# VectorE transposes head 6 as well in tiles 0 to 6, and layer 1's relu moves into the ring of block buffers

## The chip, the cores and the metric

The kernel runs on one core of one Trainium2 chip. The time is device microseconds (us) of one launch. A core has TensorE (PE: matmuls and transposes by matmul), VectorE (DVE), ScalarE (ACT), GpSimd (POOL) and SyncE (SP, which here only issues transfers), each with its own queue of instructions that it runs in order. They wait for one another through semaphores. On-chip memory is SBUF, and PSUM, where TensorE writes.

## The reference: two graph layers

There are 16 graphs of 1024 nodes with 256 features, and an integer matrix `adj` for each. Layer 0 is masked attention with 8 heads of 32 features, layer 1 is attention with a bilinear score and a leaky relu. Cut to what matters:

```
h = maximum(layernorm(x), 0)
Q, K, V = heads(h @ Wq.T + bq), heads(h @ Wk.T + bk), heads(h @ Wv.T + bv)
attn = softmax(where(adj == 0, -inf, Q @ K.T * SCALE))      # 8 heads, 1024 x 1024 each
x = x + (attn @ V) @ Wo.T + bo
h = maximum(layernorm(x), 0)
e = leaky_relu((h * a_0) @ h.T, 0.2)                         # a_1.. for adj == 2, 3, 4
x = x + softmax(where(adj == 1, e, -9e15)) @ h
```

## The kernel before

**Tiles and steps.** A graph is cut into 8 tiles of 128 rows (`t` = 0 to 7), so there are 128 tiles. The order of the work is written out by hand (lines 834 to 973). One step `s` of the loop works on three stages at once: `now`, layer 0 for tile `s`; `edge`, layer 1 for the tile 9 places back; `piece`, norm and projections for the tile 9 places ahead. A step has eight places, `h` = 0 to 7, and each engine's queue gets its instructions in the order of the calls.

**One head.** At place `h` the scores of head `h` are made by two matmuls of 128x512 (`scores`, L460) into one of two PSUM areas, `sides[0]` for heads 0, 1, 2, 3, 5 and 7 and `sides[1]` for 4 and 6. Layer 1's scores of the step also go to `sides[1]`. VectorE then masks the scores, finds the row's extreme and writes them to an SBUF buffer `p` (`softmax_max`, L472). At the next place ScalarE takes the exponential (`softmax_exp`, L489), at the place after that the 128x1024 tile is transposed into `pT`. Last, `combine(g)` (L525) multiplies the transposes of four heads with the values: group 0 at place 7 of the same step, group 1 (heads 4 to 7) at place 3 of the next step. Its 64 matmuls go round the four heads, so its third one already needs head 6.

**Two ways to transpose.** `turn` (L491) lets TensorE do it: eight 128x128 transposes (L589) into PSUM, and two copies out of it (L590), by ScalarE for heads 2, 3, 6, 7. `turn_blocks` (L497) lets VectorE transpose 32x32 blocks (L381) into a buffer `blocks`, and `place_blocks` (L386) issues four transfers of 128 KB on SP's queue, which put the blocks in their places in `pT`. The table `BY_BLOCKS` (L28) and `MIXED` (L27) say which heads of a tile go by blocks: heads 0, 1, 4, 5 in tiles 1 to 6, heads 4 and 5 in tile 0, heads 0 and 1 in tile 7. Layer 1's tile always goes by blocks (L686, L689).

**The order of the keys.** The block way wants a row's columns in another order inside a chunk of 128 than the other way. Keys and values of heads 0, 1, 4, 5 lie in that order already. Where a head's way differs from `MIXED`, `softmax_exp` (L481 to L488) takes a second buffer from the ring of `p` and the exponential reorders as it writes.

**Place 0 and place 1**, which the change touches: at place 0 of a step `turning` is the previous tile and `th` is 6. TensorE's order there is scores of head 0 (L460), the eight transposes of head 6 (L589), layer 1's first half (L625, L631); at place 1 scores of head 1, transposes of head 7, L564 and L267; then scores of head 2. VectorE's order is L472 of head 0, the block transposition of layer 1 (L381), L472 of head 1. SP's order is the transfers of head 4 and of head 5 (from places 6 and 7 of the step before), with L551 between them, then those of layer 1, then those of head 0.

**Rings.** A tag with `bufs=n` is a ring: a new tile takes a buffer over from an older one, and its first instruction waits until the older tile's last use is over. `p` has four, `blocks` three, `pT` seven, and `less` (L662, which holds layer 1's relu from L663 until GpSimd subtracts it in L674) one of its own.

Of the kernel before, what the change touches and what calls it, by code (L numbers as in the profile page):

```python
# [8 lines left out]
F32 = mybir.dt.float32  # L9
# [8 lines left out]
P = 128  # L18
HEADS = 8
HD = 32  # L20
# [4 lines left out]
NEG_INF = -9000000000000000.0  # L25
MASKED = -1e30
MIXED = (0, 1, 4, 5)  # L27
BY_BLOCKS = {7: (0, 1), 0: (4, 5)}  # L28


def by_blocks(t):
    return BY_BLOCKS.get(t, MIXED)

# [14 lines left out]
def gnn_kernel(  # L48
# [19 lines left out]
    B, N, D = x.shape  # L68
    NT = N // P
# [3 lines left out]
    NB = P // HD  # L73
# [10 lines left out]
    work = ctx.enter_context(tc.tile_pool(name="work", bufs=2))  # L84
# [103 lines left out]
    class Piece:  # L188
# [11 lines left out]
        def buffer(self, i, shape, dtype=F32):  # L200
            tag = self.tags[i]
            if tag == "pT":
                return ptp.tile(shape, dtype, tag=tag, name=tag)
            bufs = {"p": 4, "blocks": 3, "halves": 2 if self.n == 1 else 4, "qt": 2, "xin": 2}.get(tag, 1)
            return work.tile(shape, dtype, tag=tag, name=tag, bufs=bufs)

        def load(self, queue=nc.gpsimd):
# [169 lines left out]
        return rows.rearrange("(k b) n -> b k n", b=NB)  # L377

    def blocks_of(p):
        blocks = work.tile([P, NB, NT, HD], F32, tag="blocks", bufs=3)  # L380
        nc.vector.transpose(blocks.rearrange("p b j q -> p j b q"), p)  # L381
        return blocks.rearrange("p b j q -> p b (j q)")

# [31 lines left out]
    class Attend:  # L415
# [81 lines left out]
        def turn_blocks(self, h):  # L497
            self.blocks = blocks_of(self.probs[h][0])
# [94 lines left out]
    class Edges:  # L593
# [65 lines left out]
        def bend(self):  # L659

            if not self.last:
                self.less = work.tile([P, N], F32, tag="less", name="less", bufs=1)  # L662
                nc.scalar.activation(self.less, self.sel, AF.Relu, scale=1 - 1 / SLOPE)  # L663

        def leak(self):
# [20 lines left out]
        def turn_blocks(self):  # L686
            self.blocks = blocks_of(self.sel)
# [370 lines left out]
```

## Time and profile before

| what | us |
|---|---|
| median of 3 runs | 3093.83 (3088.1 to 3098.82) |
| the profiled execution's own time | 3096.04 |
| its span in the profile | 3093.7 |
| PE busy | 2966.1 (96%) |
| ACT busy | 2652.6 (86%) |
| DVE busy | 2517.3 (81%) |
| POOL busy | 2170.7 (70%) |

The profile records one execution. "Busy" is the time in which an engine had an instruction running; each row of a group of instructions gives the count, the busy time, the mean of one, and the idle time of the engine just before them with what ended it. The waits view adds up such idle time by who waited for whom. The timeline lists instructions in order of time with start and duration. Matmuls overlap each other, so their pace is read from start to start and not from the duration. SP's rows are the time it took to issue a transfer; when the data landed is recorded apart.

### The profile page before, as it was taken

To read this page: it belongs to the slowest core of one execution; us is meant where nothing else is said; L and a number is where in the kernel's file an instruction comes from. 1 tells how busy PE (TensorE), PEld (TensorE's weight loads), DVE (VectorE), ACT (ScalarE), POOL (GpSimd) and SP (SyncE) were. 2 spreads that over 40 slices of the span, in tenths; PEclk is the share of its full clock that TensorE was granted. 3 is DMA by queue.
4 is the path that set the end of the run, shared out by engine and by line. 5 is a ranking of instruction groups with operands and counts; after the bars stand their busy time and mean duration, and the time that the engine had idled before them with its cause. 6 is when DMAs were issued, how large, how long until landed. Compare 5 with 4: busy or idle time off the path is not lost. (4 is left out here: it accounts for less than half of the span.)

```text
span 3093.7 us, 96257 instructions
## 1 busy us (share of the span) xinstructions
PE 2966.1 (96%) x36722; PEld 2230.0 (72%) x36722; DVE 2517.3 (81%) x4455; ACT 2652.6 (86%) x5157; POOL 2170.7 (70%) x2995
## 2 busy tenths in 40 slices
PE   6889999999999999999999999999999999999997
PEld 3667777777777777777777777777777777777663
DVE  3777888888887888888888888888888888888884
ACT  3888988988998988988888898988888888898872
POOL 2666777777777777777777777777777777776542
PEclk8999999999999999999999999999999999999999
DMA  5676777777777777777867777777777867777653
GB/s 202 206 218 216 225 243 230 249 214 235 236 224 251 218 237 236 225 244 230 256 209 236 235 227 253 219 240 233 222 244 226 261 209 231 239 224 236 193 163 99
DMA packets 597828, 695.68 MB, mean 225 GB/s; under 512 B 63280, under 2 KB 528560, under 8 KB 597360
## 3 DMA queue, kind: packets, MB, share of 16 engines
q1 hardware_dynamic: 528288, 477.29, 51.6%
q0 software_dynamic: 66960, 210.04, 20.9%
q8 instruction: 295, 4.83, 0.7%
q10 hardware_dynamic: 2112, 2.10, 0.2%
q14 instruction: 173, 1.42, 0.1%
HBM read 252.98 MB, written 134.22 MB: 125 GB/s over the span
## 5 line engine op out<-in xcount | busy, mean ns | idle before, releaser
L472 DVE CUSTOM_DVE_ANT_0 p<-s,neg 128x1024 f32<-128x1024 f32 x1024 | 1236.2, 1208 | 238.1 <-PE s L460 191.8
L489 ACT ACTIVATE p<-p,nmx 128x1024 f32<-128x1024 f32 x1024 | 1249.4, 1223 | 146.2 <-DVE nmx L472 143.0
L460 PE MATMUL s<-k,qt 128*128 128x512 f32 x2048 | 760.5, 452 | 34.7 <-DMA qt<-qd 15.0
L590 ACT COPY pT<-trp 128x512 f32<-128x512 f32 x1024 | 548.8, 590 | 91.8 <-PE trp L589 91.6
L589 PE MATMUL trp<-ident,p 128*128 128x128 f32 x4608 | 604.4, 274 | 3.7 <-ACT pT L590 1.5
L589 PEld LDWEIGHTS trp<-ident,p 128*128 128x128 f32 x4608 | 531.7, 140 | 102.3 <-issue 10.9
L381 DVE STREAM_TRANSPOSE blocks<-p 128x1024 f32<-128x1024 f32 x456 | 564.5, 1238 | 13.5 <-ACT p L678 10.6
L525 PE MATMUL acc<-pT,v 128*32 128x128 f32 x16384 | 532.9, 275 | 37.5 <-ACT recT L519 25.8
L525 PEld LDWEIGHTS acc<-pT,v 128*32 128x32 f32 x16384 | 452.4, 110 | 148.3 <-ACT recT L519 80.8
L440 POOL TENSOR_SCALAR neg<-adj 128x1024 bf16<-128x1024 int32 x128 | 467.7, 3654 | 81.4 <-ACT neg L452 72.2
L696 PE MATMUL acc<-h,pT 128*32 128x256 f32 x8192 | 493.0, 382 | 7.9 <-DVE ot L705 7.8
L460 PEld LDWEIGHTS s<-k,qt 128*128 128x128 f32 x2048 | 322.6, 191 | 129.4 <-issue 44.3
L696 PEld LDWEIGHTS acc<-h,pT 128*32 128x32 f32 x8192 | 241.0, 109 | 210.2 <-issue 62.7
L674 POOL TENSOR_TENSOR sel<-sel,less 128x1024 f32<-128x1024 f32 x120 | 286.7, 2389 | 70.3 <-ACT less L663 49.2
L631 PE MATMUL s<-h1T,ha 128*128 128x512 f32 (+2 forms) x744 | 272.8, 490 | 2.6 <-ACT h1T L568 0.5
L672 POOL TENSOR_SCALAR less<-top 128x1 f32<-128x1 f32 x120 | 31.6, 264 | 275.4 <-DVE top L654 275.4
L324 POOL DMA_DIRECT2D qd<-halves x240 | 177.0, 777 | 58.7 <-POOL halves L314 31.7
L489 ACT ACTIVATION_READ_ACCUMULATOR p<-p,nmx 128x1 f32 x1024 | 206.2, 201 | 0.0
L509 POOL COPY wide<-rec 128x256 f32<-128x256 f32 x128 | 53.7, 419 | 210.5 <-DVE rec L507 210.5
L330 POOL DMA_DIRECT2D kd<-halves x240 | 171.7, 764 | 35.4 <-POOL halves L314 35.4
L314 POOL TENSOR_TENSOR halves<-full,halves 128x256 fp32r<-128x256 f32 x240 | 176.5, 736 | 20.6
L631 PEld LDWEIGHTS s<-h1T,ha 128*128 128x128 f32 x744 | 126.6, 190 | 70.6 <-issue 45.2
(121 smaller groups left out, 4322.6 us busy)
## 6 DMA issues: line engine op xcount, KB each, us to landing
pT<-blocks SPq DMA_DIRECT2D x2304, 128.0 KB, 3.5
k<-kd SPq DMA_DIRECT2D x128, 512.0 KB, 7.3
qt<-qd SPq DMA_DIRECT2D x128, 512.0 KB, 4.5
adj<-in_adj POOLq DMA_DIRECT2D x127, 512.0 KB, 4.9
qd<-halves POOLq DMA_DIRECT2D x240, 256.0 KB, 2.8
kd<-halves POOLq DMA_DIRECT2D x240, 128.0 KB, 4.0
xb<-in_x POOLq DMA_DIRECT2D x128, 128.0 KB, 4.2
x1d<-x SPq DMA_DIRECT2D x128, 128.0 KB, 3.9
```

Of the source, the lines that this page charges most:

```text
L324: nc.gpsimd.dma_start(out=qds[self.b][self.first, oc].rearrange("p u w n -> p u (w n)"), in_=halves.unsqueeze(1).to_broadcast([P, 2, 2 * P]),)
L381: nc.vector.transpose(blocks.rearrange("p b j q -> p j b q"), p)
L440: nc.gpsimd.tensor_scalar(self.neg, self.adj, 0.0, MASKED, ALU.is_equal, ALU.mult)
L460: nc.tensor.matmul(self.ps[:, cols], lhsT=self.qt[:, h, :], rhs=keysets[self.b][h][:, cols], start=True, stop=True,)
L472: nc.vector.tensor_tensor_reduce(out=p, in0=sides[h in (4, 6)], in1=self.neg, scale=-SCALE, scalar=FLOOR, op0=ALU.add, op1=ALU.min, accum_ ...
L489: nc.scalar.activation(to, of, AF.Exp, bias=nmx, scale=-1.0, accum_out=self.sums[:, h : h + 1])
L525: nc.tensor.matmul(sums_place[r * HD : (r + 1) * HD, g * P : (g + 1) * P], lhsT=vs[self.b][:, j, place_of(h) : place_of(h) + HD], rhs=self ...
L589: nc.tensor.transpose(tr[:, j, :], p[:, jj * P : (jj + 1) * P], ident)
L590: copy(pT[:, half * 4 : half * 4 + 4, :], tr)
L631: nc.tensor.matmul(self.side[:, cols], lhsT=self.ha[:, c, :], rhs=h1T[:, c, cols], start=(c == 0), stop=(c == NC - 1),)
L674: nc.gpsimd.tensor_tensor(self.sel, self.sel, self.less, ALU.subtract)
L696: nc.tensor.matmul(sums_place[a * HD : (a + 1) * HD, :], lhsT=self.pT[:, j, a], rhs=h1s[self.b][:, j, :], start=(j == 0), stop=(j == NT - 1),)
```

## The change

Head 6 of tiles 0 to 6 of each graph is transposed by VectorE in blocks. Head 6 is not in `MIXED`, so its exponential now writes to a second `p` buffer in the other order. The relu of layer 1 loses its own buffer and takes its place in the ring `blocks`, which has four buffers in place of three, so the memory used is the same.

```diff
-BY_BLOCKS = {7: (0, 1), 0: (4, 5)}
+BY_BLOCKS = {7: (0, 1), 0: (4, 5, 6), 1: (0, 1, 4, 5, 6), 2: (0, 1, 4, 5, 6), 3: (0, 1, 4, 5, 6), 4: (0, 1, 4, 5, 6), 5: (0, 1, 4, 5, 6), 6: (0, 1, 4, 5, 6)}
...
-            bufs = {"p": 4, "blocks": 3, "halves": 2 if self.n == 1 else 4, "qt": 2, "xin": 2}.get(tag, 1)
+            bufs = {"p": 4, "blocks": 4, "halves": 2 if self.n == 1 else 4, "qt": 2, "xin": 2}.get(tag, 1)
...
-        blocks = work.tile([P, NB, NT, HD], F32, tag="blocks", bufs=3)
+        blocks = work.tile([P, NB, NT, HD], F32, tag="blocks", bufs=4)
...
-                self.less = work.tile([P, N], F32, tag="less", name="less", bufs=1)
+                self.less = work.tile([P, N], F32, tag="blocks", name="less", bufs=4)
```

In the built queues, 112 groups of eight transposes and their 224 copies on ScalarE are gone (7 tiles of 16 graphs), and VectorE has 112 more block transpositions and SP 448 more transfers. At place 0 the new transposition stands on VectorE between L472 of head 0 and layer 1's block transposition, and on SP the new transfers stand between those of head 5 and those of layer 1.

## The prediction

> **What bounds the kernel now.** I read the page's busy times and groups, then the waits, then the timeline of one step, engine by engine. The groups that the change moves, on the page (count, busy us, mean ns, idle before them and what ended it):
>
> ```profile
> PE 2966.1 (96%) x36722; PEld 2230.0 (72%) x36722; DVE 2517.3 (81%) x4455; ACT 2652.6 (86%) x5157; POOL 2170.7 (70%) x2995
> ...
> L489 ACT ACTIVATE p<-p,nmx 128x1024 f32<-128x1024 f32 x1024 | 1249.4, 1223 | 146.2 <-DVE nmx L472 143.0
> ...
> L590 ACT COPY pT<-trp 128x512 f32<-128x512 f32 x1024 | 548.8, 590 | 91.8 <-PE trp L589 91.6
> L589 PE MATMUL trp<-ident,p 128*128 128x128 f32 x4608 | 604.4, 274 | 3.7 <-ACT pT L590 1.5
> ...
> L381 DVE STREAM_TRANSPOSE blocks<-p 128x1024 f32<-128x1024 f32 x456 | 564.5, 1238 | 13.5 <-ACT p L678 10.6
> ```
>
> PE is busy 96% and hardly waits: it sets the pace, and the change takes work from it. What that is worth depends on the place the work is taken from, so I look at the start of one step of tile t = 5, first on PE (start, duration):
>
> ```profile
> 1461.62 0.73 PE L460 MATMUL s<-k,qt 128*128 128x512 f32 x2
> 1462.19 1.04 PE L589 MATMUL trp<-ident,p 128*128 128x128 f32 x8
> 1463.06 0.60 PE L625 MATMUL s<-ident,mirror 128*128 128x128 f32 x4
> 1463.77 0.73 PE L460 MATMUL s<-k,qt 128*128 128x512 f32 x2
> ...
> 1466.24 0.71 PE L460 MATMUL s<-k,qt 128*128 128x512 f32 x2
> ...
> 1470.24 2.33 PE L525 MATMUL acc<-pT,v 128*32 128x128 f32 x64
> ```
>
> The row L589 at 1462.19 goes; it holds PE for 0.87 us, start to start. The three L460 are the scores of heads 0, 1 and 2, all into the same PSUM area. VectorE over the same time:
>
> ```profile
> 1461.05 1.24 DVE L381 STREAM_TRANSPOSE blocks<-p 128x1024 f32<-128x1024 f32 x1
> 1462.48 1.23 DVE L472 CUSTOM_DVE_ANT_0 p<-s,neg 128x1024 f32<-128x1024 f32 x1 [0.19 <-issue]
> ...
> 1463.63 1.24 DVE L381 STREAM_TRANSPOSE blocks<-sel 128x1024 f32<-128x1024 f32 x1
> 1464.80 1.19 DVE L472 CUSTOM_DVE_ANT_0 p<-s,neg 128x1024 f32<-128x1024 f32 x1
> ```
>
> L472 of head 0 ends at 1463.71, and the scores of head 1 start at 1463.77: they must not overwrite what VectorE still reads. PE's weight load shows that this is a wait already:
>
> ```profile
> 1463.77 0.30 PEld L460 LDWEIGHTS s<-k,qt 128*128 128x128 f32 x2 [0.35 <-DVE nmx L472]
> ```
>
> So from the scores of head 0 to those of head 1 a step needs 2.15 us whatever PE does between: 0.86 until L472 starts, 1.23 for it, 0.06 back. It takes 2.15 now in steps 4 to 7 and 2.34, 2.55, 2.76 in steps 3, 2, 1. (These and all places below are counted from the step's first L460, medians of 13 graphs, steps by the t of their own tile.)
>
> SP's queue over the same stretch (each row the issues of consecutive transfers):
>
> ```profile
> 1460.08 2.53 SPq L386 DMA_DIRECT2D pT<-blocks  x4
> 1462.65 0.62 SPq L551 DMA_DIRECT2D x1d<-x  x1
> 1463.37 8.90 SPq L386 DMA_DIRECT2D pT<-blocks  x12
> ```
>
> The twelve are head 5, layer 1 and head 0, back to back at 0.65 to 0.75 us each: between 1460 and 1472 SP has no room. Nor have the DMA engines much; in the windows view their share is 0.90 in the first 5 us of the step:
>
> ```profile
> 1461.40:1466.50 5.10, 4.99 (x47) 4.28 (x39) 4.69 (x8) 4.69 (x10) 3.85 (x9) 1.00 0.90 293
> ```
>
> **What is removed.** 112 x 0.87 = 97 us of PE. By the 2.15 us above, in steps 4 to 7 none of it can be used before head 1's scores, in steps 1, 2, 3 only 0.61, 0.40, 0.19. ACT loses 112 pairs of copies, 0.95 us each start to start, 106 us.
>
> **The exponential of head 6** writes in another order. In 64 of the 1024 L489 it does so now (heads 4, 5 of tile 7, heads 0, 1 of tile 0): these take 2.23 us, the others 1.16. There elements go 16 bytes apart, in the new ones 128 bytes, which no row shows. Bounds: 1.16 and 2.23; I take 2.23, the same kind of write. [...] By the row ACT gains 112 x 1.07 = 120 us of work and loses 106, and it idles 2 to 4 us in these steps. The second `p` buffer is the one that head 4 leaves, so this exponential waits for VectorE's transposition of head 4, which ends at -1.7; it starts 1.2 later than now, ends near +0.4, and the exponential of head 7 ends at 2.1, where PE wants it at 2.7. Cost 0; it begins beyond some 0.6 us of delay.
>
> **VectorE** gets one L381 more between L472 of head 0 and layer 1's L381. A start-to-start sum for the scores of head 2: 0.86 (L472 starts) + 1.15 (L472) + 1.16 (L381, new) + 1.17 (L381) + 1.23 (L472 of head 1) + 0.06 = 5.63. They start now at 5.53, 5.21, 4.90, 4.62, 4.62, 4.62, 4.62 in steps 1 to 7. PE cannot do anything else meanwhile, its order is fixed. So PE is later by 0.10, 0.42, 0.73 and four times 1.01: 5.29 a graph, 16 x 5.29 = **85 us**. Here the removed work has turned into waiting.
>
> **The transfers.** `combine(1)` in place 3 needs head 6 in its third matmul. Now that is at 10.16, 9.43, 9.12, 8.84, 8.84, 8.66, 8.74 (steps 1 to 7). The block way is ready on VectorE at about 3.2, but SP is still issuing head 5, and head 6's four take the slots that layer 1's four have now. Those are issued from about 5.05 on and the last of them has landed at 9.96, 10.15, 10.60, 10.98, 10.56, 10.54, 10.75. I take these as head 6's landings. With VectorE's delay alone the third matmul would come at 10.26, 9.85, 9.85, 9.85, 9.85, 9.67, 9.75. The later of both, less its place now, is 0.10, 0.72, 1.48, 2.14, 1.72, 1.88, 2.01: 10.05 a graph. After `combine(1)` PE's chain is packed to the next step, so the delay stays: 16 x 10.05 = **161 us**. Bounds: the tenth and ninetieth percentile of those landings are 9.94 and 11.24, the median 10.54; at 9.94 little but the VectorE term is left, at 11.24 some 0.7 x 6 x 16 = 67 us come on top.
>
> [...] The row that decides is SP's: the issue cannot be early.
>
> **The rest.** Layer 1's transfers land some 3 us later, near 13.5; their reader L696 starts after 14. Those of heads 0 and 1 are read at place 7, beyond 20; the queries (L427) land 19 after the step's start now and would land at 22, needed at 24: cost 0, with 2 us of cover. Relu in the ring: it waits for the transfers of the block tile four before it, head 5's, which have landed at 8.3 while the relu starts near 9; VectorE's head 1 (L381 at 11.3, then later) waits for head 6's landing, 10.7. Cost 0. Its own buffer made it wait for nothing, so nothing is gained either.
>
> **Sum.** Profiled execution 3096.0 + 161 = **3257 us** (5.2% over it; its own time is 2 us over the median of the runs shown).
>
> **Rivals.**
> (a) *The transfers come in time*, because PE's own lateness shifts load or SP is quicker; only VectorE's wait stays: 3096 + 85 = 3181. Against it: SP's unbroken row of issues.
> (b) *Transfers are later still*: 448 more in the busiest stretch (DMA share 0.90), so that head 6 lands at the ninetieth percentile or beyond: 3324 and more. For it: landings of L386 take 2.5 to 7.1 us now.
> (c) *Faster*: PE keeps setting the pace and the 97 us come off: 2999. It needs scores of heads 1 and 2 that do not wait for VectorE. It decides from the point where L472 of head 1 ends before PE's own work brings it to head 2's scores, which by the rows is at 3.74 to 4.66 without L589, against 5.57. For it: PE's 96%. Against: the weight load's wait, and VectorE's order.
> (d) *No change*: a gain in steps 1 to 3 that makes up for a loss far below (a).
>
> **Chances.** Forecast 0.60, (a) 0.17, (b) 0.18, (c) 0.03, (d) 0.02. The range takes (a) and the upper landing bound: 3180 to 3330. Faster by over 0.3% (9 us, about what a measurement here can tell) 0.03, within 0.02, slower 0.95.
>
> **What would show it.** PE busy falls by some 98 to about 2870 while the span grows. L460 waits for L472 before head 2's scores, 1 us a step in steps 4 to 7. The waits of PE's L525 for the transfers of `pT`, 10.9 us now, grow to about 76 (16 x 4.8, the part of the 10.05 beyond VectorE's). L489's mean rises by 112 x 1.07 / 1024 = 0.12 to 1.34 us. Wrong: if head 2's scores start before 5.6, VectorE's sum is wrong; if L525's waits stay near 10, rival (a) holds; if ACT's L489 ends up what L589 of head 7 waits for, the strided write is dearer than I took it.

## The result and the profile after

The changed kernel takes 3251.2 us (median of 4 runs, 3246.4 to 3256.7), beside 3091.3 for the one before on the same chip: ratio 1.0508, 95% interval 1.0493 to 1.0523. It is 160 us slower; the forecast was 161. The profiled execution took 3246.4, its span is 3244.5. The page's rows that answer to those shown of before, with TensorE's L460 and L525 added:

```profile
PE 2939.0 (91%) x35826; PEld 2155.6 (66%) x35826; DVE 2636.9 (81%) x4567; ACT 2652.8 (82%) x4933; POOL 2169.5 (67%) x2995
...
L489 ACT ACTIVATE p<-p,nmx 128x1024 f32<-128x1024 f32 x1024 | 1362.6, 1334 | 295.3 <-DVE nmx L472 156.6
...
L460 PE MATMUL s<-k,qt 128*128 128x512 f32 x2048 | 755.9, 450 | 175.9 <-DVE nmx L472 156.8
L381 DVE STREAM_TRANSPOSE blocks<-p 128x1024 f32<-128x1024 f32 x568 | 703.2, 1238 | 11.0 <-ACT p L678 9.3
L525 PE MATMUL acc<-pT,v 128*32 128x128 f32 x16384 | 568.9, 276 | 76.0 <-DMA pT<-blocks 51.9
...
L589 PE MATMUL trp<-ident,p 128*128 128x128 f32 x3712 | 488.7, 274 | 3.7 <-ACT pT L590 1.5
L590 ACT COPY pT<-trp 128x512 f32<-128x512 f32 x800 | 428.0, 588 | 72.2 <-PE trp L589 70.8
```

TensorE's L589 has 896 matmuls and 116 us less, ScalarE is as busy as before to 0.2 us (14 more were forecast), VectorE has 120 us more and yet is idle for 19% as before. No engine is busy for a larger share of the time, and the kernel is slower. The last column of a row, the engine's idle time before it and what ended most of it, tells why. The same two rows of TensorE in the kernel before:

```profile
L460 PE MATMUL s<-k,qt 128*128 128x512 f32 x2048 | 760.5, 452 | 34.7 <-DMA qt<-qd 15.0
L525 PE MATMUL acc<-pT,v 128*32 128x128 f32 x16384 | 532.9, 275 | 37.5 <-ACT recT L519 25.8
```

TensorE was idle 34.7 us before its L460 and is now idle 175.9, nearly all of it waiting for VectorE's L472; before L525 it went from 37.5 to 76.0, most of it waiting for transfers of `pT`.

The same stretch as was shown of before, a step of tile t = 5, TensorE first:

```profile
1530.90 0.73 PE L460 MATMUL s<-k,qt 128*128 128x512 f32 x2
1531.47 0.60 PE L625 MATMUL s<-ident,mirror 128*128 128x128 f32 x4
1533.10 0.73 PE L460 MATMUL s<-k,qt 128*128 128x512 f32 x2 [1.03 <-DVE nmx L472]
...
1536.50 0.73 PE L460 MATMUL s<-k,qt 128*128 128x512 f32 x2 [0.70 <-DVE nmx L472]
...
1540.53 0.59 PE L525 MATMUL acc<-pT,v 128*32 128x128 f32 x4
1541.28 0.49 PE L525 MATMUL acc<-pT,v 128*32 128x128 f32 x9 [0.17 <-DMA pT<-blocks]
```

The scores of head 1 start 2.20 after those of head 0, where they started 2.15 after them with eight transposes in between: the transposes are gone and a wait of 1.03 stands in their place. The scores of head 2 start at 5.60 (4.62 before), after a second wait. L525 begins with four records and stops at the fifth. (A record is one instruction in the profile; a combine is 32 matmuls in the program and 64 records here, two for each, so the four are heads 4 and 5, and the fifth is head 6.) VectorE over the same time:

```profile
1531.81 1.22 DVE L472 CUSTOM_DVE_ANT_0 p<-s,neg 128x1024 f32<-128x1024 f32 x1 [0.24 <-PE s L460]
...
1532.96 1.24 DVE L381 STREAM_TRANSPOSE blocks<-p 128x1024 f32<-128x1024 f32 x1
1534.12 1.20 DVE L381 STREAM_TRANSPOSE blocks<-sel 128x1024 f32<-128x1024 f32 x1
1535.25 1.18 DVE L472 CUSTOM_DVE_ANT_0 p<-s,neg 128x1024 f32<-128x1024 f32 x1
```

The new row is the one at 1532.96; L472 of head 1 comes behind it and ends at 1536.43, and 0.07 later TensorE may write head 2's scores.

### The profile page after: what moved, and what is told of

It is laid out like the page before. It is cut to its first block, busy times and chain, and to the rows that moved or that the text cites. A ratio compares the mean times of both kernels' runs of the same rounds, so it can differ in the third digit from the quotient of the medians.

```text
span 3244.5 us, 95027 instructions
## 1 busy us (share of the span) xinstructions
PE 2939.0 (91%) x35826; PEld 2155.6 (66%) x35826; DVE 2636.9 (81%) x4567; ACT 2652.8 (82%) x4933; POOL 2169.5 (67%) x2995
## 5 line engine op out<-in xcount | busy, mean ns | idle before, releaser
L489 ACT ACTIVATE p<-p,nmx 128x1024 f32<-128x1024 f32 x1024 | 1362.6, 1334 | 295.3 <-DVE nmx L472 156.6
L472 DVE CUSTOM_DVE_ANT_0 p<-s,neg 128x1024 f32<-128x1024 f32 x1024 | 1234.0, 1206 | 214.8 <-PE s L460 187.8
L460 PE MATMUL s<-k,qt 128*128 128x512 f32 x2048 | 755.9, 450 | 175.9 <-DVE nmx L472 156.8
L381 DVE STREAM_TRANSPOSE blocks<-p 128x1024 f32<-128x1024 f32 x568 | 703.2, 1238 | 11.0 <-ACT p L678 9.3
L525 PE MATMUL acc<-pT,v 128*32 128x128 f32 x16384 | 568.9, 276 | 76.0 <-DMA pT<-blocks 51.9
L525 PEld LDWEIGHTS acc<-pT,v 128*32 128x32 f32 x16384 | 469.0, 110 | 206.9 <-issue 96.4
L460 PEld LDWEIGHTS s<-k,qt 128*128 128x128 f32 x2048 | 318.9, 190 | 305.1 <-DVE nmx L472 230.7
L589 PE MATMUL trp<-ident,p 128*128 128x128 f32 x3712 | 488.7, 274 | 3.7 <-ACT pT L590 1.5
L590 ACT COPY pT<-trp 128x512 f32<-128x512 f32 x800 | 428.0, 588 | 72.2 <-PE trp L589 70.8
L589 PEld LDWEIGHTS trp<-ident,p 128*128 128x128 f32 x3712 | 428.3, 141 | 86.5 <-issue 11.1
L631 PE MATMUL s<-h1T,ha 128*128 128x512 f32 (+2 forms) x744 | 271.3, 487 | 0.0
L489 ACT ACTIVATION_READ_ACCUMULATOR p<-p,nmx 128x1 f32 x1024 | 205.6, 201 | 0.0
L535 DVE TENSOR_TENSOR oT<-acc,recT 128x256 f32<-128x256 f32 x128 | 54.2, 424 | 149.7 <-ACT neg L452 63.7
```

What stands on the lines that cost most here:

```text
L460: nc.tensor.matmul(self.ps[:, cols], lhsT=self.qt[:, h, :], rhs=keysets[self.b][h][:, cols], start=True, stop=True,)
L472: nc.vector.tensor_tensor_reduce(out=p, in0=sides[h in (4, 6)], in1=self.neg, scale=-SCALE, scalar=FLOOR, op0=ALU.add, op1=ALU.min, accum_ ...
L489: nc.scalar.activation(to, of, AF.Exp, bias=nmx, scale=-1.0, accum_out=self.sums[:, h : h + 1])
L525: nc.tensor.matmul(sums_place[r * HD : (r + 1) * HD, g * P : (g + 1) * P], lhsT=vs[self.b][:, j, place_of(h) : place_of(h) + HD], rhs=self ...
L589: nc.tensor.transpose(tr[:, j, :], p[:, jj * P : (jj + 1) * P], ident)
L590: copy(pT[:, half * 4 : half * 4 + 4, :], tr)
```

## The experiments

Times are medians in us; "before" was run beside each group. The numbers of the experiments are those of their labels (there is no E6 and no E8). Two causes were to be told apart and sized: VectorE's round trip ahead of head 2's scores, and the landing of head 6's transfers; against them stood the ring, the dearer exponential, and the traffic as such.

**E1: the ring alone.**

```diff
-BY_BLOCKS = {7: (0, 1), 0: (4, 5, 6), 1: (0, 1, 4, 5, 6), 2: (0, 1, 4, 5, 6), ...
+BY_BLOCKS = {7: (0, 1), 0: (4, 5)}
```

> Head 6 is transposed by TensorE as before; of the change only the ring is left (four block buffers, layer 1's relu among them). Theory of the two waits (VectorE's round trip before head 2's scores, the landing of head 6's transfers): the ring costs nothing, 3091 us as before, within 6. Rival 'ring': the relu and the block tiles wait for one another; then most of the 160 us stay, 3150 to 3250.

Measured 3092.2 beside 3091.7, ratio 0.9998 (0.9988 to 1.0007). The relu's place in the ring costs and gains nothing.

**E2: the reordering exponential alone.**

```diff
-                if turning and th in by_blocks(turning.t):
+                if turning and th != 6 and th in by_blocks(turning.t):
```

> The change without VectorE's transposition and without its transfers: head 6 of tiles 0 to 6 still goes through TensorE, but its exponential writes to a second buffer in the other order, as in the change. The columns of head 6 no longer match the values, so this part of the output is other than the reference's; the work is the same. Theory: 3091 us, at most 3120, because ScalarE idles 2 to 4 us a step and the exponential ends just before TensorE wants it. Rival 'exponential': the 112 dearer exponentials are on the path, 112 x 1.07 = 120 us, 3211.

Measured 3112.7, ratio 1.0079 (1.0062 to 1.0096): 21 us, a sixth of the 120 us that ScalarE has more to do. The scores of heads 1 and 2 come 0.05 to 0.2 later here, since TensorE's transposes of head 6 stand right behind the longer exponential (the weight loads of L589 wait 48.8 us for L489, 113 times). In the change these transposes are gone, so the 21 us should be an upper bound of what the exponential costs there; that is an argument, not a measurement.

**E3: VectorE's transposition alone**, beside TensorE's.

```diff
+                if turning and th == 6 and turning.t < NT - 1:
+                    turning.turn_blocks(th)
                 if turning and th in by_blocks(turning.t):
```

(with `BY_BLOCKS` as in E1)

> The kernel before with the ring of the change, and VectorE transposes head 6 of tiles 0 to 6 as well, into a block buffer that nobody reads; TensorE's transposes, the exponential and the transfers are those of before, so only VectorE has more to do. Theory: VectorE's round trip alone, head 2's scores at 5.6 us in steps 1 to 7, 16 x 5.2 = 83 us, 3174 (3165 to 3185). Rival 'room': VectorE is idle 19% and takes 112 x 1.16 us without a delay, 3091. Rival 'throughput': VectorE's added time counts in full, 112 x 1.16 = 130, 3221.

Measured 3154.7, ratio 1.0210 (1.0193 to 1.0227): 63 us, where 83 were expected. Head 2's scores start at 5.56 in each of steps 1 to 7, within 0.07 of the sum. Most of the missing 20 us is told below.

**E4: head 6 last in the second combine.**

```diff
+            order = [(j, r) for j in range(NT) for r in range(GROUP)]
+            if g == 1 and self.t < NT - 1:
+                others, behind = ([jr for jr in order if (jr[1] == 2) == x] for x in (False, True))
+                order = others[:12] + [jr for two in zip(behind, others[12:]) for jr in two] + others[20:]
+            for j, r in order:
...
```

> The change, with the matmuls of the second combine in another order: head 6 comes in after 12 matmuls of the three other heads, some 0.7 us later, so that its transfers have landed. Theory: the wait for the transfers (4.3 us a graph) goes, VectorE's stays: 3091 + 83 = 3174 (3170 to 3190; a few us more if the new order of the matmuls runs slower). Rival 'load': 448 more transfers slow everything, and the order of one group of matmuls changes nothing, 3240 to 3251.

Measured 3246.6, ratio 1.0515 (1.0497 to 1.0532): no gain. This did not decide anything. L525's wait for the transfers fell from 51.9 us to 10.7, but the new order is slower by itself: from the combine's first matmul to TensorE's next instruction took at least 2.58 us in steps of t = 5, beside 2.09 in the kernel before. The wait was paid back in matmuls.

**E5: layer 1's transposition later.** VectorE's wait is taken away, the landing stays.

```diff
-                    if edge_was:
-                        edge_was.turn_blocks()
-                        edge_was.place_blocks()
                 if h == 1:
...
                         was.reciprocals()
+                    if edge_was:
+                        edge_was.turn_blocks()
+                        edge_was.place_blocks()
```

> The change, with layer 1's block transposition and its transfers moved from place 0 to place 1, behind VectorE's work on head 1 and the reciprocals. Between the scores of heads 0 and 2 VectorE then has one transposition, as before. Theory: VectorE's wait goes (head 2's scores at 4.7 to 5.0 in place of 5.6), but head 6's transfers land where they landed, near 10.3, and TensorE now waits for them in full: the two waits lie in a row before one point, so that taking away the first alone gives little, 3235 to 3251. Rival 'the waits add up': 3251 - 83 = 3168.

Measured 3255.2, ratio 1.0529 (1.0512 to 1.0547), the changed kernel's time. Its waits of TensorE (time in total, times, longest):

```profile
PE acc L525 <- DMA pT<-blocks: 119.7, 103, 2.2
PE s L460 <- DVE nmx L472: 80.9, 97, 1.6
```

The changed kernel's two rows were

```profile
PE s L460 <- DVE nmx L472: 156.8, 196, 1.6
PE acc L525 <- DMA pT<-blocks: 51.9, 82, 2.0
```

Head 2's scores start at 4.67 again, 0.94 earlier than in the change, and TensorE waits longer at the combine: what one row loses the other nearly gains (76 and 68 us). The two waits do not add up; the later one sets the time.

**E9: no wait for the landing.**

```diff
-                        rhs=self.turned[h][:, j],
+                        rhs=self.turned[7 if h == 6 and self.t < NT - 1 else h][:, j],
```

> The change, but the second combine of tiles 0 to 6 reads head 7's transposition in head 6's place; head 6's transfers are issued and land as in the change, and nobody waits for them. This part of the output is wrong, the order and the sizes of all instructions are those of the change. Theory: the wait for the landing goes (4.3 us a graph, 16 x 4.3 = 68), VectorE's stays: 3251 - 68 = 3183 (3165 to 3190). Rival 'load': the transfers cost by their traffic, not by their landing, 3240 to 3251.

Measured 3151.9, ratio 1.0200 (1.0183 to 1.0217): 99 us less than the change, not 68, and 61 above before, as E3. The transfers run as in the change (the last of head 6 lands at 10.1 to 10.6). E3, in which head 6 has no transfers, is 63 above before, so traffic without the wait costs nothing that could be seen here.

**E10: neither wait**, the edits of E5 and E9.

> Both edits: layer 1's transposition at place 1, and head 7's transposition read in head 6's place (that part of the output is wrong). Theory: both waits are gone, and TensorE gains what the 2.15 to 2.2 us between the scores of heads 0 and 1 leave of the removed transposes, in steps 1 to 3 alone: 16 x 0.9 = 14 us, 3077 (3065 to 3092). Rival 'load': some 50 to 100 us stay over the time before. Rival 'TensorE alone': the 97 us come off in full, 2994.

Measured 3099.8, ratio 1.0031 (1.0021 to 1.0040). All of the 160 us but 9 are gone, and none of TensorE's 97 us has come off. Head 1's scores start at 2.19 to 2.21 in steps 1 to 7 (2.15 to 2.76 before): the round trip of head 0 is the floor, as forecast. The gain of steps 1 and 2 (0.79 and 0.23 us) is given back by 0.08 to 0.38 in the steps after, where TensorE does nothing new and yet is later; part of that is L460 waiting for ScalarE's L645 (5.6 us in all), the rest was not taken apart. So the 14 us of the forecast for this run did not come.

**E11: head 6's transfers from ScalarE's queue.**

```diff
                 if ending:
                     ending.softmax_exp(eh)
+                if h == 1 and was and 6 in by_blocks(was.t):
+                    was.place_blocks(6, nc.scalar)
...
                 if turning and th in by_blocks(turning.t):
                     turning.turn_blocks(th)
-                    turning.place_blocks(th)
+                    if th != 6:
+                        turning.place_blocks(th)
```

> The change, with head 6's four transfers issued from ScalarE's queue in place of SP's, in place 1 behind the exponential of head 0. They can be issued from about 3.7 to 6.1 us of the step on, where SP issues them from 5.1 to 7.7. Theory 'SP's order': they land 1.4 us earlier, near 8.9, before the second combine wants them at 9.85; the 99 us of the landing wait go, less what 2.4 us of issuing on ScalarE put before its copy for that combine (0 to 0.5 us a step, up to 56): 3152 to 3208. Rival 'full transfer engines': they are 0.90 busy in that stretch, an earlier issue only stands in line, landing after 10, 3235 to 3260.

Measured 3550.7, ratio 1.1440 (1.1391 to 1.1488), far outside what either theory expected. ScalarE's rows and those of its queue (ACTq) in one step that starts at 1684.26:

```profile
1687.82 0.58 ACTq L386 DMA_DIRECT2D pT<-blocks  x1
...
1688.44 3.62 ACTq L386 DMA_DIRECT2D pT<-blocks  x3
1692.24 1.07 ACT L590 COPY pT<-trp 128x512 f32<-128x512 f32 x2 [4.13 <-DMA pT<-blocks]
...
1695.73 0.38 ACT L519 COPY recT<-acc 128x256 f32<-128x256 f32 x1
```

The issues took 0.58, 1.31, 0.95 and 1.29 us, and ScalarE computed nothing for 4.13. L519, which the second combine needs, came at 11.5, beside some 9.2 in the change. The landings do not settle the question that the run was to answer. Medians of steps 1 to 7, from the step's start, for head 6's four transfers:

| | issued at | landed at |
|---|---|---|
| the change, from SP | 5.08, 5.80, 6.58, 7.22 | 8.31, 8.91, 9.95, 10.34 |
| E11, from ScalarE | 3.54, 4.21, 5.39, 6.78 | 8.18, 9.24, 10.23, 11.43 |

The first two went out 1.5 to 1.6 earlier and landed at most 0.1 earlier, which speaks for full engines. But the last, for which the combine would have waited, was issued only 0.4 earlier (and landed 1.1 later), and SP meanwhile issued layer 1's four from 5.26 on, where the change has them from 7.92 on, so that more transfers were under way at once. What an earlier issue would do by itself is not shown.

**E12: half of the bytes.**

```diff
-                out=pT[:, a * NT * HD : (a + 1) * NT * HD], in_=blocks[a * HD : (a + 1) * HD]
+                out=pT[:, a * NT * HD : a * NT * HD + n * HD], in_=blocks[a * HD : (a + 1) * HD, :, : n * HD]
```

(with n = 4 for head 6 and 8 for the others; for head 6 of tiles 0 to 6 the second combine reads `self.turned[h][:, j % 4]`)

> The change, but head 6's four transfers move only half of the columns (4 of 8 blocks; the second combine reads these four twice, so this part of the output is wrong); number, queue and place of the issues are those of the change. Theory 'SP's order': the landing is set by the issue, it stays within 0.3 us, 3225 to 3251. Rival 'full transfer engines': 256 KB less before the landing are some 0.9 us at the 293 GB/s of that stretch, so that little of the wait is left, 3152 to 3180.

Measured 3202.9 beside 3096.3, ratio 1.0348 (1.0331 to 1.0365), between the two expectations: 107 us over before, where the change is 160 over it. With the same issues from 4.7 to 5.4 on, the last transfer landed at 9.5 to 9.8 in place of 10.2 to 10.4, some 0.65 earlier, and 53 us came off. So the issue alone does not set the landing; the bytes count too. SP's order still holds the larger part: the last of the four is issued at 7.2, and the fastest of all transfers of L386 in the change takes 2.4 us from issue to landing, so that without any load this one would land at some 9.6 (an estimate from these two numbers), 0.7 before it does. Whether fewer bytes shorten the transfer itself or its wait behind others is not shown.

**E7: head 2 in place of head 6.** The same amounts of work, in another place.

```diff
-BY_BLOCKS = {7: (0, 1), 0: (4, 5, 6), 1: (0, 1, 4, 5, 6), ...
+BY_BLOCKS = {7: (0, 1), 0: (2, 4, 5), 1: (0, 1, 2, 4, 5), ...
```

> Head 2 goes by blocks in place of head 6, in tiles 0 to 6; all else is as in the change. Its transposition stands in place 4, where heads 4 and 5 use different PSUM areas, so that no scores wait for VectorE there, and where SP's queue is nearly empty; the transfers are read 6 us later, in the first combine of place 7. Theory: the same amounts of work as the change, but TensorE's 0.87 us are usable, less some 0.3 us for the second half of place 4 and perhaps some wait in the first combine: 112 x 0.3 to 0.87, 3091 - 60 = 3030 (2995 to 3070). Rival 'amounts': a head by blocks costs what it costs, wherever it stands, 3200 or more. Rival 'late landing': the transfers land after the first combine wants them, 3091 to 3150.

Measured 3543.3, ratio 1.1441 (1.1366 to 1.1516): 453 us slower, where 60 faster was expected. I had looked at PSUM and SP's queue in place 4, and not at the rest. ScalarE, then TensorE, in a step that starts at 1663.11:

```profile
1670.91 2.10 ACT L489 ACTIVATE p<-p,nmx 128x1024 f32<-128x1024 f32 x1 [1.51 <-DVE blocks L381]
```

```profile
1673.28 2.16 PE L525 MATMUL acc<-pT,v 128*32 128x128 f32 x64 [1.54 <-ACT recT L519]
...
1687.19 2.63 PE L525 MATMUL acc<-pT,v 128*32 128x128 f32 x60 [2.21 <-DMA pT<-blocks]
```

Head 2's exponential needs the second `p` buffer, which head 0's transposition on VectorE leaves only then; it starts 1.51 late and takes 2.10, and L519 stands behind it on ScalarE, so the second combine waits 1.54. And head 2's transfers, issued behind the queries' from 1680.64 on, land at 1687.06, while the first combine wants them at 1684.6. Over the run TensorE's L525 waits 280.8 us for transfers and 166.5 for L519, together 411 us more than before (10.9 and 25.8), most of the 453. So the amounts decide nothing (the same amounts cost 160 in one place and 453 in another), but the place that I had picked as free was not.

No version that ran beats the kernel before.

## Why the prediction was right, and where its steps were not

**Right: the floor under TensorE's gain.** The 2.15 us between head 0's and head 1's scores are a round trip through one PSUM area. E10 shows it: with both losses taken away and 97 us of TensorE's work gone, head 1's scores start at 2.2 in every step, and the time is that of before plus 9.

**Right: VectorE's sum for head 2's scores.** 5.63 was forecast; 5.60 or 5.61 in every one of steps 1 to 7.

**Too high: what that sum costs.** The forecast had 85 us; alone it cost 63 (E3) and 61 (E9). Two parts of the 24 us can be read from the spans of single graphs. In steps 1 to 7 of the first graph there is no layer 1 yet, so only one transposition stands between the two L472: that graph lost 0.0 us in E3 and gained 1.2 in E9, where 5.3 were counted. And the chain behind is not packed in every step: in E9 the steps 1, 6 and 7 lost -0.30, 0.86 and 0.71 us for 0.10, 1.01 and 1.01. In 6 and 7 the same is seen in E3 (0.82, 0.72): TensorE met waits there anyway, and arriving later it met less of them. Step 1 is another matter, for in E3 it lost 0.01: in E9 ScalarE has no copies of head 6, and in a step of t = 1 its L568 came 0.8 earlier and TensorE's L631, which needs it, 0.59 after head 2's scores in place of 0.85. In the steps 3 to 5 the loss is as worked out (0.72, 1.00, 0.99). I had called TensorE's chain packed, and in steps 2 to 5 it is.

**Too low: the landing's share.** The forecast had 161 - 85 = 76 us; E9 makes it 99. On graphs 2 to 16 it is 5.4 us a graph, near the 4.8 counted; on the first graph alone it is 14.7 (13.5 lost in the change, 1.2 gained in E9), which I had put down like the others. There the third matmuls of the second combine came 7.9 us later in all than in E9, and TensorE's clock was at half for 17.0 us after the graph's first step, beside 3.4 in E9, which is worth at most half of the difference, 6.8 us (an estimate). Three of the four stretches at half follow a wait of 1.6 us of L267 for ScalarE's L250, which the kernel before has too, so that part need not belong to the landing. The landings, taken from layer 1's rows, were right within 0.8: 10.2 to 10.4 in the medians by step, forecast 10.0 to 11.0. Steps 3 and 4 were put too late, and from the measured places of the third matmul the sum of both waits is 9.4 us a graph in place of 10.05. So the total of 161 for a measured 160 is luck in part: two errors of some 23 us cancel.

**Right: only the later of two waits counts.** The sum took the later of VectorE's and the transfers' time in each step. The four combinations show it: both waits 3251, without VectorE's 3255, without the landing's 3152, without either 3100. Taking away VectorE's alone is worth nothing, and with the landing's gone it is worth 52.

**Right in part: why the transfers cannot be earlier.** The step said that SP's row decides, since SP's queue is full. By the numbers under E12 SP's order accounts for a landing at some 9.6 of the 10.3, but half of the bytes with the same issues landed 0.65 earlier, and in E11 two transfers issued 1.5 to 1.6 earlier landed at most 0.1 earlier, with others beside them. So the load of the transfer engines, whose share of 0.90 stands beside SP's row in the prediction, has a part as well. Rival (a), in which the transfers come in time, gave 85 for the whole; measured are 160. The last transfer was issued 2.6 us before TensorE wanted it (7.2, and 9.85 in E9), and the fastest of L386 took 2.4 from issue to landing, which leaves 0.2 for any load beside it.

**Right: ScalarE.** The mean of L489 is 1.334 us (forecast 1.34), the 176 exponentials that reorder take 2.21 on average, and L589 of head 7 does not wait for them (1.1 us in all for its weight loads, 0.4 for its matmuls). That the new ones, with 128 bytes between elements, cost what those with 16 cost is now measured (2.21 beside 2.23 us); the forecast had put them at 2.23 without a row that showed it.

**Wrong: what the profile would show of TensorE's busy time.** It fell by 27 us to 2939, not by 98 to 2870. Rows that wait in the middle of a group count as busy: L525's busy time rose by 36 us with not one matmul more, and without the landing's wait (E9) TensorE is busy for 2894.5. That explains 44 of the 71 us between 2939 and the forecast; the other 26 were not taken apart. For the same reason the row of L525's waits shows 51.9 us, where 76 were forecast and 99 measured as time.

**Left open.** What ScalarE's dearer exponential costs inside the change was not taken apart from the two waits; E2 gives 21 us where TensorE's transposes stand behind it, and E10, which has it, is 9 above before. Whether an earlier landing by another way (larger transfers, fewer bytes from others, another order on SP's queue) would make the change pay was not tried; E9 and E10, in which nobody waits for the landing, are still 61 and 9 above before.

## What to carry to other kernels

Work taken from the engine that sets the pace is worth something only up to the next point where that engine waits for another (in E10 none of TensorE's 97 us came off): look for the round trip around the place from which it is taken, and price the relief by what is left of it. Where the moved work goes, ask who stands behind it in that engine's queue, and when its result lands in the busiest stretch rather than on average; two waits before one point cost the later one, so taking away the one that ends earlier gained nothing (E5, 3255 beside 3251), and taking away the later gained only what lay beyond the earlier (E9, 99 of the 160 us). And a place that looks free on the engine and the queue that were looked at has to be checked on all the others, as E7 shows: transfers that landed late, ScalarE's order and one buffer of a ring turned an expected gain of 60 us into a loss of 453.

## What the runs showed of the hardware that was not expected

**In E7 TensorE's clock fell behind a wait of 2.2 us, far from the longest of L525 (6.7).** The step shown has TensorE idle from 1684.98 to 1687.19. The windows view of that kernel (after the busy times: granted clock, DMA share, GB/s):

```profile
1684.90:1689.70 4.80, 2.59 (x62) 2.21 (x60) 2.50 (x4) 2.46 (x6) 4.08 (x10) 0.85 0.96 289
1689.70:1692.00 2.30, 2.30 (x12) 1.96 (x11) 0.89 (x1) 0.14 (x1) 1.14 (x2) 0.57 1.01 332
```

The clock is 1.00 in the windows before and at half for 3.4 us from 1688.3 on, while TensorE works again; 60 records of L525 take 2.63 us there, where 62 took 1.95 in the kernel before. In all it is at half for 298 us in E7 and for 333 in E11, beside some 59 in the change, so a part of their losses is this and not the waits themselves. Of the 3.4 us before the fall, as long as the stretch at half itself, TensorE was idle for 2.2. In the change less stands before it: on its first graph, behind the first step, the clock falls to half four times, each time after 3.4 us in which TensorE was idle for 1.7 to 1.8. From 219 us on it stays at 1.0 to the last 9 us, although one wait of L525 lasts 2.0. What a wait needs to bring it about was not tested.

**Issuing from ScalarE held up that engine.** On SP an issue of L386 took 0.60 us in the median in the change. On ScalarE in E11 the four of a step took 0.55, 0.74, 0.90 and 0.89 in the median, up to 1.31 in the step shown, and the compute behind them waited, 4.13 us there. The transfer engines' share was 0.98 in that step from 1684.3 to 1687.8 and 0.93 from there to 1692.1; in the same parts of the change's step it was 0.90 and 0.87. Why the issues took longer was not tested.
